# LayerNorm scales a unit two units behind its squares, and the gates are computed for a whole pair of images

## The chip, the core and the metric

The kernel runs on one core of a Trainium2 chip. The metric is the time of one execution in microseconds of the device. Five engines take part, each with its own instruction queue: TensorE (PE), VectorE (DVE), ScalarE (ACT), GpSimd (POOL) and SyncE (SP), which here only issues transfers (DMA). The engines wait for each other through semaphores.

## The reference

The program computes two layers in float32 on an input of 32 images with 128 channels and 56 x 56 pixels (100,352 tokens). Only the first layer matters here. It ends in a mixture of eight experts, and the routing needs what the changed stage computes.

```python
x = conv_depthwise_7x7(input) + dw_bias          # NCHW, then one token per pixel
mu, var = x.mean(-1), x.var(-1)                  # over the 128 channels
x = (x - mu) / sqrt(var + 1e-6) * ln_gamma + ln_beta
logits = x @ Wg + bg                             # 8 experts
topv, topi = top_k(logits, 2)
wts = softmax(topv)
order = argsort(-wts[:, 0])                      # the tokens by the first weight
# each expert takes its first 15,680 tokens in that order, computes
# gelu(x @ W1 + b1) @ W2 + b2, and adds it, weighted, to its tokens
x = input + x + layer_scale * moe
```

The second layer (coordinate attention and a 3 x 3 convolution) follows and is not touched.

## The kernel before

The kernel runs in stages that follow each other: the depthwise convolution (up to 670 us), LayerNorm with the gates (694 to 1226 us), the routing of expert 0 (to 1327 us), the experts with the rest of the routing (to about 3320 us), and the second layer. The change touches the second stage only, L175 to L309.

**Units.** A pair of images has 6272 tokens, 49 on each of the 128 partitions. The 16 pairs are each cut into two units: unit (i, 0) has 24 tokens per partition and unit (i, 1) 25. One unit passes through these steps:

- `centre` (L211): with the first unit of a pair, SP loads the images of the next pair (`lnyt`, L216; two buffers). Then, in groups of three tokens, PE multiplies each token with `proj` (L227). That gives the centred token, 128 values, and its eight unscaled logits in one PSUM tile (`lnps`, eight buffers). ACT copies the group to `cen` in SBUF (L228, three buffers of one unit) and squares it: in unit (i, 0) one token at a time with a running sum into `var` (L232), in unit (i, 1) a group at a time into `sqs` (L234, one buffer).
- `spread` (L236): in unit (i, 1) DVE sums the squares (L239). POOL turns `var` into the reciprocal root `rstd` by two instructions (L240, L241).
- `normalise` (L243): DVE scales each token by `rstd` and gamma into the row buffer `xn` (L250, one instruction per token, four buffers of one unit) and the logits (L253, L254). Then it searches for the two best experts (L260 to L269): maximum, comparison, rank, second maximum. This is a chain in which nearly every instruction needs the one before it.
- `exp` (L272): one ACT instruction.
- `gates` (L276 to L292): ten more DVE instructions and the expert index (L288) write the weights into the row and the priorities into `prio` (L292). SP stores the rows in `acc_d` (L294).

**What sets the order.** The loop at L299 puts the steps of different units beside each other: in turn k it calls `centre` of unit k, `exp` of unit k-2, `normalise` of unit k-1, `spread` of unit k and `gates` of unit k-2. A scheduler then orders the instructions of each engine by its own estimate of when they can start, which mixes the steps of a turn; every engine works its queue strictly in that order. On DVE, the scheduler sets the scales of one unit between the search and the gates of another. Buffers add waits: a unit's copies to `cen` wait until the unit that had the buffer has been read by L253, and the first scale of a unit waits until the rows that lay in its `xn` buffer are stored.

**Behind the stage.** The routing counts over all of `prio` (L407), so it begins when the last L292 is done. POOL clears a tile for a zero fill of `acc_d` (L579) when the last rows have been stored.

Of the kernel before, what the change touches and what calls it, by code (L numbers as in the profile page):

```python
# [21 lines left out]
E = 8  # L22
CAP = int(1.25 * T / E)
FF = 4 * C
P = 128
# [20 lines left out]
def bc(ap, shape):  # L46
    return ap.to_broadcast(shape)
# [3 lines left out]
def moe_conv_then_coordatt_kernel(ctx: ExitStack, tc: tile.TileContext, a: dict, out: bass.AP):  # L51
# [122 lines left out]

    with ExitStack() as st:  # L175
        yp = st.enter_context(tc.tile_pool(name="lny", bufs=2))
        cp1 = st.enter_context(tc.tile_pool(name="lnc", bufs=3))
        xp = st.enter_context(tc.tile_pool(name="lnx", bufs=4))
        sp = st.enter_context(tc.tile_pool(name="lns", bufs=3))
        pp = st.enter_context(tc.tile_pool(name="lnp", bufs=8, space=PSUM))  # L180
        halves = ((0, TPP // 2), (TPP // 2, TPP))
        U = TPP - TPP // 2
        rank_e = sp.tile([P, E], F32, name="rank_e", bufs=1)
        for e in range(E):
            nc.gpsimd.memset(rank_e[:, e : e + 1], float(E - e))
        one_u = sp.tile([P, U], F32, name="one_u", bufs=1)
        nc.gpsimd.memset(one_u, 1.0)
        all_e = sp.tile([P, U], F32, name="all_e", bufs=1)
        nc.gpsimd.memset(all_e, float(E))
        yts = {}  # L190

        class Unit:
# [12 lines left out]
            def over_tokens(self, x):  # L205
                return bc(x.unsqueeze(1), [P, self.n, E])

            def over_experts(self, x):
                return bc(x.unsqueeze(2), [P, self.n, E])

            def centre(self):  # L211

                if self.h == 0:
                    for i in range(len(yts), min(self.i + 2, NPAIR)):
                        yt = yp.tile([C, 2, HW], F32, tag="yt", name=f"lnyt{i}")
                        nc.sync.dma_start(yt, y_d[2 * i : 2 * i + 2].rearrange("n c f -> c n f"))  # L216
                        yts[i] = yt.rearrange("c n f -> c (n f)").rearrange("c (p j) -> c j p", j=TPP)
                yf = yts[self.i]
                self.cen = self.tile(cp1, "cen", [P, U, C + E])
                self.var = self.tile(sp, "var")  # L220
                if self.h == 1:
                    self.sq = cp1.tile([P, U, C], F32, tag="sqs", name=f"sqs{self.nm}", bufs=1)[:, 0 : self.n]
                for g in range(0, self.n, 3):
                    m = min(3, self.n - g)
                    ps = pp.tile([P, 3, C + E], F32, tag="ps", name=f"lnps{self.nm}_{g}")
                    for j in range(m):
                        nc.tensor.matmul(ps[:, j, :], lhsT=yf[:, self.j0 + g + j, :], rhs=proj, start=True, stop=True)  # L227
                    nc.scalar.copy(self.cen[:, g : g + m, :], ps[:, 0:m, :])  # L228
                    if self.h == 0:
                        for j in range(m):  # L230
                            sq = sp.tile([P, C], F32, tag="sq", name=f"sq{self.nm}_{g}_{j}")
                            nc.scalar.activation(sq, ps[:, j, 0:C], AF.Square, accum_out=self.var[:, g + j : g + j + 1])  # L232
                    else:
                        nc.scalar.activation(self.sq[:, g : g + m, :], ps[:, 0:m, 0:C], AF.Square)  # L234

            def spread(self):  # L236
                self.rstd = self.tile(sp, "rstd")
                if self.h == 1:
                    nc.vector.tensor_reduce(self.var, self.sq, AX.X, ALU.add)  # L239
                nc.gpsimd.tensor_scalar(self.var, self.var, 1.0 / C, 1e-6, ALU.mult, ALU.add)  # L240
                nc.gpsimd.tensor_tensor(self.rstd, self.var, bc(mhalf, [P, self.n]), ALU.pow)  # L241

            def normalise(self):  # L243

                n = self.n
                self.row = self.tile(xp, "xn", [P, U, RW])
                xn = self.row[:, :, 0:C]
                rstd = self.rstd
                for j in range(n):
                    nc.vector.scalar_tensor_tensor(xn[:, j, :], self.cen[:, j, 0:C], rstd[:, j : j + 1], gamma_bc,  # L250
                                                   ALU.mult, ALU.mult)
                l = self.tile(sp, "lgs", [P, U, E])
                nc.vector.tensor_tensor(l, self.cen[:, :, C : C + E], self.over_experts(rstd), ALU.mult)  # L253
                nc.vector.tensor_tensor(l, l, self.over_tokens(logit_c), ALU.add)  # L254
                t = self.tile(sp, "gt", [P, U, E])
                self.oh = [self.tile(sp, f"oh{k}", [P, U, E]) for k in range(2)]
                self.m = [self.tile(sp, f"m{k}") for k in range(2)]
                self.later, second = self.tile(sp, "later"), self.tile(sp, "second")
                for k in range(2):
                    nc.vector.tensor_reduce(self.m[k], l, AX.X, ALU.max)  # L260
                    nc.vector.tensor_tensor(t, l, self.over_experts(self.m[k]), ALU.is_equal)
                    nc.vector.tensor_tensor(t, t, self.over_tokens(rank_e), ALU.mult)
                    mx = (self.later, second)[k]
                    nc.vector.tensor_reduce(mx, t, AX.X, ALU.max)
                    nc.vector.tensor_tensor(self.oh[k], self.over_tokens(rank_e), self.over_experts(mx), ALU.is_equal)
                    if k == 0:
                        nc.vector.scalar_tensor_tensor(l, self.oh[0], -3.0e38, l, ALU.mult, ALU.add)
                nc.vector.tensor_tensor(self.m[1], self.m[1], self.m[0], ALU.subtract)
                nc.vector.tensor_tensor(self.later, self.later, second, ALU.min)  # L269

            def exp(self):
                nc.scalar.activation(self.m[1], self.m[1], AF.Exp)  # L272

            def gates(self):

                n, mx, w0, w1 = self.n, self.m[1], self.tile(sp, "w0"), self.tile(sp, "w1")  # L276
                one = one_u[:, 0:n]
                t = self.tile(sp, "gt2", [P, U, E])
                nc.vector.tensor_tensor(mx, mx, one, ALU.min)
                nc.vector.tensor_tensor(w0, mx, one, ALU.add)  # L280
                nc.vector.reciprocal(w0, w0)
                nc.vector.scalar_tensor_tensor(w0, w0, 0.5, one, ALU.max, ALU.min)
                nc.vector.tensor_tensor(w1, mx, w0, ALU.mult)
                row, oh = self.row, self.oh
                nc.vector.tensor_tensor(row[:, :, C : C + E], oh[0], self.over_experts(w0), ALU.mult)
                nc.vector.tensor_tensor(t, oh[1], self.over_experts(w1), ALU.mult)
                nc.vector.tensor_tensor(row[:, :, C : C + E], row[:, :, C : C + E], t, ALU.add)
                nc.vector.scalar_tensor_tensor(row[:, :, C + E : RW], self.later.unsqueeze(2), -1.0,  # L288
                                               all_e[:, 0:n].unsqueeze(2), ALU.mult, ALU.add)
                nc.vector.tensor_tensor(oh[1], oh[0], oh[1], ALU.add)  # L290
                cols = slice(self.i * TPP + self.j0, self.i * TPP + self.j1)
                nc.vector.tensor_tensor(prio[:, :, cols].rearrange("p e t -> p t e"), oh[1], self.over_experts(w0), ALU.mult)  # L292
                rows = slice(self.i * TPP * P, (self.i + 1) * TPP * P)
                nc.sync.dma_start(acc_d[rows, :].rearrange("(p j) c -> p j c", p=P)[:, self.j0 : self.j1, :], row)  # L294

        mhalf = sp.tile([P, 1], F32, name="mhalf", bufs=1)
        nc.gpsimd.memset(mhalf, -0.5)
# [12 lines left out]


    with ExitStack() as st:
# [759 lines left out]
```

## Time and profile before

| what | us |
|---|---|
| median of 3 runs | 4523.59 (4507.34 to 4524.99) |
| the profiled execution | 4519.41 |
| its span, first to last instruction | 4517.7 |
| first matmul of the stage | 694.48 |
| first scale of a token | 711.38 |
| last write of `prio` begins | 1225.72 |
| first gather of expert 0 | 1326.92 |
| first scatter of expert 0 | 1387.58 |

The page gives the busy time of each engine over the whole span: PE 3625.3 us (80%), DVE 2569.1 (57%), POOL 2550.8 (56%), ACT 1411.3 (31%). These shares are means over stages that differ. For one stage, the windows view gives the busy time of each engine between two times, with the number of instructions in brackets, the granted clock of PE, the share of the transfer engines and the rate in GB/s. The timeline gives, per instruction, its start, its duration, the engine, the line of the kernel, the operation, what it writes and reads, and in square brackets how long the engine had been idle and what released it. On one engine an instruction can start before the record of the one before it ends, so the distance of two starts is the time that an instruction costs, and the duration is a little more.

### The profile page before, as it was taken

Reading aid. Unit: us, or ns where it says so; the run is one execution under the profiler, and the core shown is the slowest. Engines: PE = TensorE matmul, PEld = TensorE weight load, DVE = VectorE, ACT = ScalarE, POOL = GpSimd, SP = SyncE. Lnnn points to the kernel's source line nnn. Section 1 sums busy time; section 2 is a strip of 40 time slices with the busy share of each in tenths; the row PEclk is TensorE's granted clock in tenths of the full one; section 3 lists DMA queues with packets and bytes.
Section 4 is the critical chain, followed back from the end, with each engine's and each line's share of the span. In section 5 each row is a group of like instructions: output and inputs, shape, how many; then the busy total and the mean of one; then the engine's idle time right before and its main releaser. Section 6 shows DMA issues by size and latency. Waiting matters only on the chain. (4 is left out here: it accounts for less than half of the span.)

```text
span 4517.7 us, 59987 instructions
## 1 busy us (share of the span) xinstructions
PE 3625.3 (80%) x21360; PEld 2369.6 (52%) x21360; DVE 2569.1 (57%) x5914; ACT 1411.3 (31%) x3132; POOL 2550.8 (56%) x1983
## 2 busy tenths in 40 slices
PE   9999998676328896788788446697958999999899
PEld 4555448676316665565565334464634544455444
DVE  1111115888866966886743112232358888888786
ACT  1111115555203432334243222343412333333232
POOL 1000102232217777668677437777769787877775
PEclk9999998787658898798898778898979999999999
DMA  9999995545362121111111111111155555555552
GB/s 172 217 230 216 230 192 195 231 183 236 150 230 56 49 59 51 44 44 46 52 52 56 46 34 52 56 56 56 56 164 187 174 191 194 168 190 171 176 161 77
DMA packets 814971, 587.33 MB, mean 130 GB/s; under 512 B 545984, under 2 KB 751312, under 8 KB 802128
## 3 DMA queue, kind: packets, MB, share of 16 engines
q1 hardware_dynamic: 508816, 328.72, 25.3%
q10 hardware_dynamic: 262336, 157.84, 12.4%
q0 software_dynamic: 43264, 94.64, 7.3%
q8 instruction: 193, 3.16, 0.3%
q14 instruction: 362, 2.97, 0.2%
HBM read 320.96 MB, written 260.09 MB: 129 GB/s over the span
## 5 line engine op out<-in xcount | busy, mean ns | idle before, releaser
L591 POOL DMA_INDIRECT xg<-acc_d,idx x676 | 673.1, 996 | 408.7 <-issue 172.5
L646 POOL DMA_INDIRECT acc_d<-yo,row x676 | 717.1, 1061 | 234.8 <-issue 82.8
L612 PE MATMUL ph<-fxt,w 128*128 128x512 f32 (+1 forms) x1440 | 700.8, 631 | 53.7 <-ACT ht L613 53.7
L613 ACT ACTIVATE ht<-ph,bias 128x512 f32<-128x512 f32 (+1 forms) x720 | 489.5, 682 | 703.7 <-PE ph L612 702.6
L977 PE MATMUL pc<-v,wk 128*128 128x392 f32 x1920 | 706.1, 510 | 0.4 <-POOL v L962 0.4
L621 PEld LDWEIGHTS py<-w,ht 128*128 128x128 f32 x5728 | 664.9, 192 | 64.8 <-issue 58.2
L621 PE MATMUL py<-w,ht 128*128 128x128 f32 x5728 | 670.5, 276 | 0.0
L144 PE MATMUL acc<-xt,band 56*64 56x424 f32 (+3 forms) x7168 | 666.5, 528 | 2.7 <-POOL band L132 2.7
L144 PEld LDWEIGHTS acc<-xt,band 56*64 56x64 f32 x7168 | 337.6, 133 | 331.0 <-issue 273.3
L977 PEld LDWEIGHTS pc<-v,wk 128*128 128x128 f32 x1920 | 349.2, 192 | 308.6 <-issue 105.7
L227 PE MATMUL lnps<-proj,lnyt 128*128 128x136 f32 x1568 | 354.7, 400 | 138.8 <-ACT sq L232 71.8
L612 PEld LDWEIGHTS ph<-fxt,w 128*128 128x128 f32 x1440 | 279.5, 206 | 329.0 <-issue 243.1
L636 ACT ACTIVATE yo<-xg,own 128x137 f32<-128x137 f32 x716 | 238.0, 401 | 634.9 <-DVE own L632 369.6
L227 PEld LDWEIGHTS lnps<-proj,lnyt 128*128 128x128 f32 x1568 | 349.4, 319 | 144.6 <-ACT sq L232 74.5
L157 DVE TENSOR_SCALAR yt<-acc,dwb 128x448 f32<-128x448 f32 x128 | 87.5, 684 | 582.2 <-PE acc L144 425.2
L639 DVE TENSOR_TENSOR ys<-py,b 128x512 f32<-128x512 f32 (+2 forms) x184 | 123.8, 675 | 490.8 <-PE py L621 480.8
L602 PE MATMUL pt<-ident,xg 128*128 128x128 f32 x716 | 137.0, 311 | 329.7 <-issue 159.2
L132 POOL COPY band<-hk 56x392 f32<-56x392 f32 x128 | 65.2, 510 | 572.4 <-issue 502.0
L987 DVE SCALAR_TENSOR_TENSOR y<-pc,y 128x392 f32<-128x392 f32 x640 | 317.6, 554 | 17.7 <-PE pc L977 17.6
L957 POOL TENSOR_TENSOR d<-pad 128x3248 f32<-128x3248 f32 x32 | 228.1, 7127 | 171.2 <-DVE pad L949 171.2
L894 POOL TENSOR_TENSOR cxn<-cxn,cx 128x896 f32<-128x896 f32 x112 | 261.5, 2344 | 68.3 <-DMA cxn<-acc_d 24.5
L602 PEld LDWEIGHTS pt<-ident,xg 128*128 128x128 f32 x716 | 96.3, 161 | 357.9 <-issue 311.2
(225 smaller groups left out, 4653.8 us busy)
## 6 DMA issues: line engine op xcount, KB each, us to landing
xt<-in_x SPq DMA_DIRECT2D x128, 392.0 KB
y_d<-yt ACTq DMA_DIRECT2D x256, 196.0 KB
lnyt<-y_d SPq DMA_DIRECT2D x16, 3136.0 KB
x<-in_x SPq DMA_DIRECT2D x16, 3136.0 KB
cxn<-acc_d SPq DMA_DIRECT2D x112, 448.0 KB
cx<-acc_d SPq DMA_DIRECT2D x112, 448.0 KB
out<-y ACTq DMA_DIRECT2D x64, 784.0 KB
acc_d<-xn SPq DMA_DIRECT2D x16, 1712.5 KB
```

What stands on the lines that cost most here:

```text
L144: nc.tensor.matmul(acc[c][half * G : (half + 1) * G, :, lo:hi], lhsT=band[rows, dw, :], rhs=xt[rows, im, lo + s : hi + s], start=(n == 0), ...
L227: nc.tensor.matmul(ps[:, j, :], lhsT=yf[:, self.j0 + g + j, :], rhs=proj, start=True, stop=True)
L591: d = nc.gpsimd.indirect_dma_start(out=xg[0:n, k, :], out_offset=None, in_=acc_d[0:T1, :], in_offset=bass.IndirectOffsetOnAxis(ap=idx[0][0 ...
L602: nc.tensor.transpose(pt[:, k * P : k * P + n], xg[0:n, k, 0:C], ident[0:n, 0:n])
L612: nc.tensor.matmul(ph[:, 0:N_], lhsT=w[0][:, f * P : (f + 1) * P], rhs=xt[:, 0:N_], start=True, stop=True)
L613: nc.scalar.activation(ht[:, f, 0:N_], ph[:, 0:N_], AF.Gelu, bias=w[2][:, f : f + 1])
L621: nc.tensor.matmul(py[0:n, k, :], lhsT=ht[:, f, k * P : k * P + n], rhs=w2[:, f, :], start=(f == 0), stop=(f == NF - 1))
L636: nc.scalar.activation(yo[0:n, k, :], xg[0:n, k, :], AF.Copy, scale=own[0:n, k : k + 1])
L646: d = nc.gpsimd.indirect_dma_start(out=acc_d[:, :], out_offset=bass.IndirectOffsetOnAxis(ap=row[0:n, k : k + 1], axis=0), in_=yo[0:n, k, : ...
L894: nc.gpsimd.tensor_tensor(xn, xn, x2, ALU.add)
L977: nc.tensor.matmul(m[k], lhsT=wk[k][:, dw, :], rhs=v[:, k, rows, dw : dw + W], start=(dw == 0), stop=(dw == 2))
L987: nc.vector.scalar_tensor_tensor(r[x], m[k], f, r[y_], ALU.mult, ALU.add)
```

## The change

- `normalise` of a unit is called two turns behind its `centre` and `spread` instead of one. `cen` has four buffers instead of three.
- The search and the gates are moved from the class `Unit` to a class `Pair` and work on all 49 tokens of a pair at once: the search in the turn behind, the gates one turn later. Their work tiles have one buffer each instead of three.
- The row buffer holds a pair, in two buffers (four of one unit before), and the rows of a pair are stored by one transfer.
- The single squares of ACT share one buffer `sq` instead of three. `sqs` moves to a pool of its own, with one buffer as before.
- The loop runs one turn longer.

The core of the diff, with the calls of the loop:

```diff
-        cp1 = st.enter_context(tc.tile_pool(name="lnc", bufs=3))
-        xp = st.enter_context(tc.tile_pool(name="lnx", bufs=4))
+        cp1 = st.enter_context(tc.tile_pool(name="lnc", bufs=4))
+        qp = st.enter_context(tc.tile_pool(name="lnq", bufs=1))
+        xp = st.enter_context(tc.tile_pool(name="lnx", bufs=2))
...
+        class Pair:
+            def tile(self, pool, tag, shape=None):
+                return pool.tile(shape or [P, TPP], F32, tag=tag, name=f"{tag}{self.i}", bufs=2 if pool is xp else 1)
+            def open(self):
+                self.row = self.tile(xp, "xn", [P, TPP, RW])
+                self.l = self.tile(sp, "lgs", [P, TPP, E])
+            def top(self):
+                l, n = self.l, TPP
+                nc.vector.tensor_tensor(l, l, over_tokens(logit_c, n), ALU.add)
...
+            def gates(self):
...
+                nc.sync.dma_start(acc_d[rows, :].rearrange("(p j) c -> p j c", p=P), row)
...
-                            sq = sp.tile([P, C], F32, tag="sq", name=f"sq{self.nm}_{g}_{j}")
+                            sq = sp.tile([P, C], F32, tag="sq", name=f"sq{self.nm}_{g}_{j}", bufs=1)
...
             def normalise(self):
...
+                pair = pairs[self.i]
+                if self.h == 0:
+                    pair.open()
+                for j in range(self.n):
+                    nc.vector.scalar_tensor_tensor(pair.row[:, self.j0 + j, 0:C], self.cen[:, j, 0:C],
+                                                   self.rstd[:, j : j + 1], gamma_bc, ALU.mult, ALU.mult)
+                nc.vector.tensor_tensor(pair.l[:, self.j0 : self.j1, :], self.cen[:, :, C : C + E],
+                                        over_experts(self.rstd, self.n), ALU.mult)
...
-        for k in range(len(units) + 2):
+        for k in range(len(units) + 3):
+            pair = pairs[(k - 3) // 2] if k >= 3 else None
             if k < len(units):
                 units[k].centre()
-            if k >= 2:
-                units[k - 2].exp()
-            if 1 <= k <= len(units):
-                units[k - 1].normalise()
+            if pair and k % 2 == 0:
+                pair.exp()
             if k < len(units):
                 units[k].spread()
-            if k >= 2:
-                units[k - 2].gates()
+            if 2 <= k <= len(units) + 1:
+                units[k - 2].normalise()
+            if pair:
+                (pair.top if k % 2 else pair.gates)()
```

In the changed kernel the first line of the search is L218, the gates' last write of the row is L250, the reduction is L303, the scale L312 and the logits L314. The bodies of `top` and `gates` hold the same instructions as before, over 49 tokens.

More of the change, by code (lines that the diff above doesn't have):

```diff
@@ L182, in moe_conv_then_coordatt_kernel @@
         U = TPP - TPP // 2
+        NSQ = TPP // 2
         rank_e = sp.tile([P, E], F32, name="rank_e", bufs=1)
@@ L185, in moe_conv_then_coordatt_kernel @@
             nc.gpsimd.memset(rank_e[:, e : e + 1], float(E - e))
-        one_u = sp.tile([P, U], F32, name="one_u", bufs=1)
-        nc.gpsimd.memset(one_u, 1.0)
-        all_e = sp.tile([P, U], F32, name="all_e", bufs=1)
+        one_t = sp.tile([P, TPP], F32, name="one_t", bufs=1)
+        nc.gpsimd.memset(one_t, 1.0)
+        all_e = sp.tile([P, TPP], F32, name="all_e", bufs=1)
         nc.gpsimd.memset(all_e, float(E))
+        mhalf = sp.tile([P, 1], F32, name="mhalf", bufs=1)
+        nc.gpsimd.memset(mhalf, -0.5)
@@ L190, in moe_conv_then_coordatt_kernel, with over_tokens, over_experts, __init__ @@
         yts = {}
+        def over_tokens(x, n):
+            return bc(x.unsqueeze(1), [P, n, E])
+        def over_experts(x, n):
+            return bc(x.unsqueeze(2), [P, n, E])
+        class Pair:
+            def __init__(self, i):
+                self.i = i
+            def tile(self, pool, tag, shape=None):
[6 more added lines that the diff above has]
+                nc.vector.tensor_tensor(l, l, over_tokens(logit_c, n), ALU.add)
+                t = self.tile(sp, "gt", [P, TPP, E])
+                self.oh = [self.tile(sp, f"oh{k}", [P, TPP, E]) for k in range(2)]
+                self.m = [self.tile(sp, f"m{k}") for k in range(2)]
+                self.later, second = self.tile(sp, "later"), self.tile(sp, "second")
+                for k in range(2):
+                    nc.vector.tensor_reduce(self.m[k], l, AX.X, ALU.max)
+                    nc.vector.tensor_tensor(t, l, over_experts(self.m[k], n), ALU.is_equal)
+                    nc.vector.tensor_tensor(t, t, over_tokens(rank_e, n), ALU.mult)
+                    mx = (self.later, second)[k]
+                    nc.vector.tensor_reduce(mx, t, AX.X, ALU.max)
+                    nc.vector.tensor_tensor(self.oh[k], over_tokens(rank_e, n), over_experts(mx, n), ALU.is_equal)
+                    if k == 0:
+                        nc.vector.scalar_tensor_tensor(l, self.oh[0], -3.0e38, l, ALU.mult, ALU.add)
+                nc.vector.tensor_tensor(self.m[1], self.m[1], self.m[0], ALU.subtract)
+                nc.vector.tensor_tensor(self.later, self.later, second, ALU.min)
+            def exp(self):
+                nc.scalar.activation(self.m[1], self.m[1], AF.Exp)
+            def gates(self):
+                n, mx, w0, w1 = TPP, self.m[1], self.tile(sp, "w0"), self.tile(sp, "w1")
+                t = self.tile(sp, "gt", [P, TPP, E])
+                nc.vector.tensor_tensor(mx, mx, one_t, ALU.min)
+                nc.vector.tensor_tensor(w0, mx, one_t, ALU.add)
+                nc.vector.reciprocal(w0, w0)
+                nc.vector.scalar_tensor_tensor(w0, w0, 0.5, one_t, ALU.max, ALU.min)
+                nc.vector.tensor_tensor(w1, mx, w0, ALU.mult)
+                row, oh = self.row, self.oh
+                nc.vector.tensor_tensor(row[:, :, C : C + E], oh[0], over_experts(w0, n), ALU.mult)
+                nc.vector.tensor_tensor(t, oh[1], over_experts(w1, n), ALU.mult)
+                nc.vector.tensor_tensor(row[:, :, C : C + E], row[:, :, C : C + E], t, ALU.add)
+                nc.vector.scalar_tensor_tensor(row[:, :, C + E : RW], self.later.unsqueeze(2), -1.0, all_e.unsqueeze(2),
+                                               ALU.mult, ALU.add)
+                nc.vector.tensor_tensor(oh[1], oh[0], oh[1], ALU.add)
+                cols = slice(self.i * TPP, (self.i + 1) * TPP)
+                nc.vector.tensor_tensor(prio[:, :, cols].rearrange("p e t -> p t e"), oh[1], over_experts(w0, n), ALU.mult)
+                rows = slice(self.i * TPP * P, (self.i + 1) * TPP * P)
+                nc.sync.dma_start(acc_d[rows, :].rearrange("(p j) c -> p j c", p=P), row)
@@ L192, in moe_conv_then_coordatt_kernel @@
+        pairs = [Pair(i) for i in range(NPAIR)]
         class Unit:
@@ L203, in tile @@
                 return t[:, 0 : self.n]
[L205 to L209, printed above, removed]
             def centre(self):
@@ L220, in centre @@
                 self.var = self.tile(sp, "var")
-                if self.h == 1:
-                    self.sq = cp1.tile([P, U, C], F32, tag="sqs", name=f"sqs{self.nm}", bufs=1)[:, 0 : self.n]
+                self.alone = 0 if self.h else NSQ
+                if self.alone < self.n:
+                    self.sq = qp.tile([P, U, C], F32, tag="sqs", name=f"sqs{self.nm}")
                 for g in range(0, self.n, 3):
@@ L228, in centre @@
                     nc.scalar.copy(self.cen[:, g : g + m, :], ps[:, 0:m, :])
-                    if self.h == 0:
+                    if g < self.alone:
                         for j in range(m):
-                            sq = sp.tile([P, C], F32, tag="sq", name=f"sq{self.nm}_{g}_{j}")
+                            sq = sp.tile([P, C], F32, tag="sq", name=f"sq{self.nm}_{g}_{j}", bufs=1)
                             nc.scalar.activation(sq, ps[:, j, 0:C], AF.Square, accum_out=self.var[:, g + j : g + j + 1])
@@ L237, in spread @@
                 self.rstd = self.tile(sp, "rstd")
-                if self.h == 1:
-                    nc.vector.tensor_reduce(self.var, self.sq, AX.X, ALU.add)
+                if self.alone < self.n:
+                    nc.vector.tensor_reduce(self.var, self.sq[:, 0 : self.n], AX.X, ALU.add)
                 nc.gpsimd.tensor_scalar(self.var, self.var, 1.0 / C, 1e-6, ALU.mult, ALU.add)
@@ L243, in normalise @@
             def normalise(self):
[L245 to L294, printed above, removed]
@@ L296, in moe_conv_then_coordatt_kernel @@
-        mhalf = sp.tile([P, 1], F32, name="mhalf", bufs=1)
-        nc.gpsimd.memset(mhalf, -0.5)
+                pair = pairs[self.i]
[6 more added lines that the diff above has]
+                                        over_experts(self.rstd, self.n), ALU.mult)
```

## The prediction

> **What bounds the kernel now.** The stage between the depthwise convolution and the routing, 694.5 to 1226.1 us, is the only one whose code changes. It ends when the last write of `prio` (L292, 1225.72 + 0.4) lets the routing count begin. First view: busy time by window, for the stage and for one period of it, a pair of images (two units of 24 and 25 tokens).
>
> ```profile
> core 0: us, PE busy (x) PEld busy (x) DVE busy (x) ACT busy (x) POOL busy (x), PEclk, DMA share, GB/s
> 694.48:1226.14 531.66, 356.57 (x1576) 351.19 (x1576) 447.96 (x1645) 270.98 (x1216) 150.59 (x82) 0.78 0.48 193
> ...
> 820.63:852.52 31.89, 22.30 (x99) 21.90 (x99) 27.84 (x103) 16.77 (x76) 9.21 (x4) 0.73 0.52 210
> ```
>
> Read the second line: a pair takes 31.89 us; DVE works 27.84 of them, PE 22.30, ACT 16.77, POOL 9.21. DVE bounds it and loses 4.05 us. Where, says DVE's timeline around the pair's border, and POOL's beside it:
>
> ```profile
> 812.26 3.49 DVE L239 TENSOR_REDUCE var<-sqs 128x25 f32<-128x3200 f32 x1
> 815.65 0.35 DVE L254 TENSOR_TENSOR lgs<-lgs,logit_c 128x192 f32<-128x192 f32 x1
> ...
> 816.42 0.17 DVE L280 TENSOR_TENSOR w<-m,one_u 128x25 f32<-128x25 f32 x1
> 820.63 0.35 DVE L250 SCALAR_TENSOR_TENSOR xn<-cen,rstd,gamma_bc 128x128 f32<-128x128 f32 x1 [4.05 <-POOL rstd L241]
> ```
>
> ```profile
> 815.83 0.38 POOL L240 TENSOR_SCALAR var<-var 128x25 f32<-128x25 f32 x1 [22.43 <-DVE var L239]
> 816.29 4.31 POOL L241 TENSOR_TENSOR rstd<-var,mhalf 128x25 f32<-128x25 f32 x1
> 820.68 0.37 POOL L240 TENSOR_SCALAR var<-var 128x24 f32<-128x24 f32 x1
> 821.14 4.15 POOL L241 TENSOR_TENSOR rstd<-var,mhalf 128x24 f32<-128x24 f32 x1
> ```
>
> DVE sums the squares (L239), POOL needs 0.38 + 4.31 us for the root, and the scale (L250) that wants it stands a few instructions behind. The list of waits gives the same wait 100.5 us in 17 times: 33.9 at the stage's start, about 4.2 in each pair.
>
> **The change part by part.**
>
> *Scale two units behind.* In the built program's order, the reduction of unit (p+2, 1) now stands in the gates of pair p, a whole pair ahead of its scale. The 4.7 us of POOL lie beside some 27 us of DVE work: -4.05 per pair. Its cover would have to shrink below 4.7 us to bring any of it back.
>
> *Gates for a pair at once.* 25 instructions per unit (12 wide and 2 narrow in the search, 5 wide, 5 narrow and the expert index in the gates) become 25 per pair, twice as wide. DVE starts: 200 elements 0.273 us after the last, 192 0.265, 25 elements 0.09, 3200 elements 3.39 (812.26 to 815.65). So about 1.04 ns an element and 0.065 us per instruction: 25 x 0.065 = -1.6 us per pair.
>
> *What the order adds.* Before, the scheduler put a scale or a gate between most dependent instructions. After, ten of the pair's search (its first to its tenth wide instruction) directly follow the one they need. The routing's chain shows the price:
>
> ```profile
> 1228.01 0.16 DVE L419 TENSOR_SCALAR enough_r<-ps_r 128x1 f32<-128x1 f32 x1 [0.66 <-PE ps_r L408]
> 1228.09 0.14 DVE L421 TENSOR_SCALAR mid_r<-thr_r 128x1 f32<-128x1 f32 x1
> ...
> 1230.31 0.16 DVE L419 TENSOR_SCALAR enough_r<-ps_r 128x1 f32<-128x1 f32 x1 [0.68 <-PE ps_r L408]
> 1230.50 0.16 DVE L420 TENSOR_TENSOR thr_r<-thr_r,enough_r 128x1 f32<-128x1 f32 x1
> ```
>
> An independent neighbour starts 0.08 later, a dependent one 0.19: its predecessor's end and 0.03. A wide one shows the same (L254 at 1215.87 for 0.36, L260 at 1216.27). So 10 x 0.12 = +1.2 us per pair; bounds 0 and 25 x 0.12 = 3.0. The Trainium skill (VectorE: DVE Perf Modes, The DRAIN you can't avoid) says that a semaphore between chained Vector instructions costs nothing extra; by it this term would be 0 and the whole 4442. I keep the rows.
>
> The period is then 27.84 - 1.6 + 1.2 = **27.4 us** instead of 31.9.
>
> *Does another engine become the bound?* POOL's two roots, 9.2 us, now run wholly beside DVE. The second of them does already (821.14 to 825.29), and there DVE's two-input instructions start 0.26 to 0.28 apart as elsewhere: price 0, upper bound the 8.5 us of both. The Trainium skill (SBUF — State Buffer, Who interferes with whom) says that a Vector instruction with two SBUF inputs and a GpSimd instruction that reads SBUF lock each other out; by it up to 8.5 us per pair would come back, 14.5 x 8.5 = 123, and the whole would be an estimated 4583. The row speaks against it.
>
> PE needs 0.442 us a token (244 records, 122 tokens, in the 53.94 us from 694.48), 21.7 a pair. It waits for PSUM: ACT may copy a unit only when one of four `cen` buffers is free. With L314 of (p, 0) at 0 and of (p, 1) at 13.7, ACT copies and squares (p+2, 0) from 0, and PE refills eight groups by 13.4; those of the next unit are full 12.3 after 13.7, when 13.7 are there. So PE fits, by 0.3 us once. ACT's single squares now share one buffer: back to back, each waits for the last (0.16 to issue, 0.20 to 0.22 to read the sum, 0.04) and takes 0.40 instead of 0.25; 16 of 24 do, +2.4, in ACT's 15 idle us. The exponential waits in ACT's queue ahead of one copy and its squares, for a DVE result that comes 6 us after the unit's copies start; ACT has just finished them.
>
> *The rows leave pair by pair.* SP sends 3.44 MB at once instead of 1.68 and 1.75, and two pair buffers replace four unit buffers. The first scale of pair p+1 waits for the rows of pair p-1. DVE work from their last write (L250 new) to it: 0.47 + 0.26 + 0.53 + 21 x 0.263 + 0.40 + 9 x 0.60 + 1.1 = 13.7 us. Landing: the last rows before (1.75 MB) were issued at 1225.42 and released POOL at 1232.22, 6.8 us; the queues move 432 GB/s in the window 800 to 809, 4.1 us for 1.75 MB, so about 2.7 of latency. For 3.44 MB: 8.0 + 2.7 = 10.7. No wait, 3 us spare. In SP's queue the next image load comes behind the rows; it waits for PE's last matmul of pair p+3, thus for L314 of (p+1, 1), 7.1 us behind the rows' last write, and copies and squares after it, 8.8 in all, when the rows are nearly out.
>
> *The start costs.* ACT's new order mixes the first unit's squares with the second unit's copies, paced by PE: the last square comes behind the seventh copy of unit (0, 1), at 714.62 before, so it ends at about 715.5, and the first scale stands 4.7 us behind (706.7 to 711.4 before): 720.2. Then 5 scales, a reduction, 44 scales and the first wide ones take 17.5 (737.7); pair 1's squares end at 694.5 + 98 x 0.442 + 0.6 = 738.4; their reduction, the first search and 24 scales take 15.5 (754.0). The exponential, in ACT's queue behind work that PE paces, holds DVE to some 755.5. Pair 2's squares end after 147 tokens, 694.5 + 65.0 + 0.5 = 760.0, and its reduction, which DVE reaches at about 756.4, waits for them. From there the period rules.
>
> *The sum.* Reduction of pair 2 at 760.0; of pair 15, 13 periods later, 1116.2; one period on, 1143.6, DVE stands where the next would be, and needs 10.0 us (25 scales 6.6, five wide 2.5, the rest 0.9) to the last logits, 1153.6. Then the last pair's search, 12 wide at 0.58 with routing set-up between them (7.0), and gates with the b2 product of 1.14 (5.9): 1166.5. Before it was 1226.1: **-59.6 us**. Behind it the order on every engine is the same but for the set-up; the zero fill starts some 4 us later against `prio`, with the first scatter at 1387 and thus about 75 us spare. All of it shifts. The profiled execution took 4519.4 us (span 4517.7): 4459.8. The median of the runs is 4.2 above it; I say **4460**.
>
> **The rivals.**
>
> *A better one (4442).* Dependence costs nothing: period 26.2, 14.5 x 1.2 = 17 us more. For it: most dependent neighbours in the trace are one element long, and nothing says that long ones pay as much. Against: the PE margin of 0.3 us, which a shorter period eats.
>
> *A part comes back (4475 to 4505).* PE's refill or the image load late by 1 to 3 us in each pair: 14 x (1 to 3) = 14 to 42 us. For it: PE waited twice in each pair before:
>
> ```profile
> 807.01 15.30 PE L227 MATMUL lnps<-proj,lnyt 128*128 128x136 f32 x68 [5.64 <-ACT sq L232]
> 826.34 6.99 PE L227 MATMUL lnps<-proj,lnyt 128*128 128x136 f32 x30 [4.03 <-ACT sqs L234]
> ```
>
> *The change doesn't do what it says (4505 to 4523).* The scale finds a root that is late for another reason, or the start and the fuller tail eat it. Only if a pair still costs over 31 us.
>
> *Slower (4525 to 4567).* The row buffers: if the rows share the queues with the next image load (3.21 MB), both together need 6.65 / 0.432 = 15.4, + 2.7 = 18.1 us. From 13.7 + 4.5 = 18.2 on, the new wait of the first scale in a pair is as long as the old one. At the 361 GB/s that the window 1225 to 1300 shows, it is 18.4 + 2.7 = 21.1: a wait of 7.4, period 34.8, 14.5 x 2.9 + 5 = 47 us on top, 4567. Against it: the order and the 8.8 us above.
>
> **How the numbers follow.** Forecast (4445 to 4475) 0.62; better (4430 to 4445) 0.12; part comes back 0.16, of it 0.04 above 4497; doesn't do it 0.05; slower 0.05. About 0.5%, 23 us, is what a measurement here can tell from no change: faster is below 4497, 0.62 + 0.12 + 0.12 = 0.86; the same 0.09; slower 0.05. The range holds the forecast, three quarters of the better case and two thirds of the part that comes back, 0.62 + 0.09 + 0.11 = 0.82: 4434 to 4495; it takes in the 3.0 us bound of the dependence, 1.8 x 14.5 = 26 on top, 4486.
>
> **What would show it.** A DVE period of 27.4 us with no wait for `rstd` behind the start; the search's wide instructions 0.60 apart; no wait of the scale for the rows' DMA; the first scale at 720; the count at 1166. Wrong: a period set by PE, or a scale that DMA releases.

## The result, and the profile after

| | before | after |
|---|---|---|
| median of the runs, us | 4515.47 (4 runs, 4502.84 to 4524.99) | 4465.74 (4 runs, 4459.73 to 4468.19) |
| the profiled execution's span | 4517.7 | 4466.5 |
| first matmul of the stage | 694.5 | 694.1 |
| first scale of a token | 711.4 | 719.8 |
| last reduction of squares (pair 15) | 1195.9 | 1117.0 |
| the routing count begins | 1226.2 | 1169.4 |
| the stage: first matmul to count | 531.7 | 475.3 |

The ratio after to before is 0.9883, interval 0.9859 to 0.9906. The change makes the kernel faster by 50 us in the medians and by 56 us in the stage that it touches.

Busy time by window, for the stage and for one period of it, as it was shown for before (columns: window, its length, then busy time and instructions of each engine):

```profile
core 0: us, PE busy (x) PEld busy (x) DVE busy (x) ACT busy (x) POOL busy (x), PEclk, DMA share, GB/s
694.07:1169.40 475.33, 366.06 (x1576) 352.17 (x1576) 437.71 (x1249) 288.96 (x1200) 171.16 (x84) 0.81 0.53 214
842.39:869.86 27.47, 23.20 (x98) 21.97 (x98) 27.13 (x80) 18.16 (x76) 10.79 (x4) 0.88 0.60 242
```

A pair now takes 27.47 us instead of 31.89. DVE works 27.13 of them and has lost its 4 us of idle time. It starts 77 instructions in the period instead of 102, the 25 fewer that the change takes away (the 80 and 103 in the brackets also count those that the window's ends cut). Over thirteen periods, from the reduction of pair 2 to that of pair 15, the mean is (1116.96 - 760.56) / 13 = 27.42 us; before it was (1195.94 - 780.24) / 13 = 31.98.

DVE's timeline around a pair's border answers to the two views of before that showed the wait:

```profile
1089.50 3.48 DVE L303 TENSOR_REDUCE var<-sqs 128x25 f32<-128x3200 f32 x1
...
1093.97 0.55 DVE L248 TENSOR_TENSOR xn<-oh,w 128x392 f32<-128x392 f32 x1
1094.44 0.55 DVE L249 TENSOR_TENSOR gt<-oh,w 128x392 f32<-128x392 f32 x1
...
1095.18 0.55 DVE L250 TENSOR_TENSOR xn<-xn,gt 128x392 f32<-128x392 f32 x1
...
1097.07 5.57 DVE L312 SCALAR_TENSOR_TENSOR xn<-cen,rstd,gamma_bc 128x128 f32<-128x128 f32 x21
1102.56 0.35 DVE L314 TENSOR_TENSOR lgs<-cen,rstd 128x200 f32<-128x200 f32 x1
1102.95 0.57 DVE L218 TENSOR_TENSOR lgs<-lgs,logit_c 128x392 f32<-128x392 f32 x1
1103.55 0.56 DVE L224 TENSOR_REDUCE m<-lgs 128x49 f32<-128x392 f32 x1
1104.15 0.57 DVE L225 TENSOR_TENSOR gt<-lgs,m 128x392 f32<-128x392 f32 x1
```

No line has a bracket behind it: nothing waits. The reduction (L303) belongs to a unit whose scales come a whole pair later. The search begins at L218, and its instructions, each of which needs the one before it, start 0.60 us apart. The gates' L248 and L249, as wide but independent of each other, start 0.47 apart. The list of DVE's waits over the stage (columns: who waits for what, us in all, times, longest) has no steady-state wait left:

```profile
DVE xn L312 <- POOL rstd L305: 42.7, 2, 42.5
DVE var L303 <- ACT sqs L298: 6.1, 2, 4.5
```

The 42.5 us are the stage's start. The rest is two short waits for squares there (1.66 and 4.46 us) and one of 0.24 for a root.

### The profile page after: what moved, and what is told of

Its sections match the earlier page's. It is cut to its first block, busy times and chain, and to the rows that moved or that the text cites. A ratio compares the mean times of both kernels' runs of the same rounds, so it can differ in the third digit from the quotient of the medians.

```text
span 4466.5 us, 59526 instructions
## 1 busy us (share of the span) xinstructions
PE 3636.8 (81%) x21360; PEld 2379.5 (53%) x21360; DVE 2557.9 (57%) x5514; ACT 1429.9 (32%) x3116; POOL 2578.7 (58%) x1983
## 5 line engine op out<-in xcount | busy, mean ns | idle before, releaser
L291 PE MATMUL lnps<-proj,lnyt 128*128 128x136 f32 x1568 | 364.2, 399 | 63.9 <-ACT sq L296 39.2
L915 POOL TENSOR_TENSOR cxn<-cxn,cx 128x896 f32<-128x896 f32 x112 | 260.8, 2338 | 69.3 <-PE pc L998 26.4
```

Of the source, the lines that this page charges most:

```text
L915: nc.gpsimd.tensor_tensor(xn, xn, x2, ALU.add)
```

## The experiments

The experiments ran on three chips, numbered 3, 5 and 14 in the record, each with its own runs of the kernel before; by their times, none is the chip of the runs above. There the stages behind the count take much longer (the kernel before: 5050 to 5060 us), but the changed stage takes the same time: 475.1 us for the changed kernel on chip 14, against 475.3 above. So the stage is compared across all runs, and the whole only against the kernel before on the same chip (ratio, with its 95% interval). "Period" is the mean of thirteen pairs, as above.

| kernel | stage, us | period | whole against before, interval |
|---|---|---|---|
| before | 531.7 | 31.98 | 1 |
| after (chip 14) | 475.1 | 27.41 | 0.9896 (0.9866 to 0.9926) |
| moved scale alone | 478.2 | 27.84 | 0.9892 (0.9853 to 0.9931) |
| pairs alone | 487.1 | 28.10 | 0.9907 (0.9878 to 0.9936) |
| reduction moved alone | 471.1 | 27.76 | 0.9886 (0.9858 to 0.9914) |
| search between the scales | 494.4 | 28.82 | 0.9917 (0.9892 to 0.9942) |
| the same, late reduction and products | 464.1 and 463.1 | 26.99 and 26.91 | 0.9887 (0.9842 to 0.9932) and 0.9880 (0.9856 to 0.9904) |
| late products | 473.4 | 27.42 | 0.9897 (0.9866 to 0.9928) |
| root twice | 475.4 | 27.42 | one run, no interval |
| products on GpSimd (second try) | 542.8 | 32.16 | one run, no interval |
| rows twice | 545.0 | 33.09 | one run, no interval |

**The moved scale alone.**

```diff
# on the kernel before
-        cp1 = st.enter_context(tc.tile_pool(name="lnc", bufs=3))
+        cp1 = st.enter_context(tc.tile_pool(name="lnc", bufs=4))
...
-        for k in range(len(units) + 2):
+        for k in range(len(units) + 3):
...
-                units[k - 2].exp()
-            if 1 <= k <= len(units):
-                units[k - 1].normalise()
+                units[k - 3].exp()
             if k < len(units):
                 units[k].spread()
...
+                units[k - 2].normalise()
+            if k >= 3:
+                units[k - 3].gates()
```

> The kernel before with one part of the change: normalise and gates of a unit one turn later, four cen buffers; search and gates stay per unit, the rows leave per unit (single squares share one buffer as in the change, and the two scratch tiles of search and gates have one buffer, for room). Theory (the moved scale is the gain, the pairs are worth only 0.4 us): no wait of the scale for rstd behind the start, DVE period per pair 27.8 us, first scale at about 720, count at about 1172, whole 4460 to 4475. Rival (the pairs for themselves are the gain): wait of about 4 us stays, period near 31.9, whole near 4515.

Measured: period 27.84, one wait for `rstd` (42.8, the start), stage 478.2. The theory holds: the deferral takes all of the wait away, and the pairs add only 27.84 - 27.42 = 0.4 us per pair.

**The pairs alone.**

```diff
# on the changed kernel: cen bufs=3, the loop back to one turn of delay
+            if 1 <= k <= len(units):
+                units[k - 1].normalise()
             if k < len(units):
                 units[k].spread()
-            if 2 <= k <= len(units) + 1:
-                units[k - 2].normalise()
             if pair:
-                (pair.top if k % 2 else pair.gates)()
+                (pair.gates if k % 2 else pair.top)()
```

> The changed kernel with normalise one turn behind again and three cen buffers; search, gates and rows per pair as in the change. By its order the reduction of a unit (p+2, 1) still stands ahead of a whole pair's search and 24 scales, some 13 us ahead of its own scale, since the scheduler moves it there, and seven of the ten dependent neighbours of the search get a scale between them. Theory A (the wait goes wherever 4.7 us of DVE work stand between reduction and scale, whatever moved it): no wait for rstd in the steady state, period 26.6 to 27.0, count 1150 to 1165, whole 4448 to 4465. Theory B (the scale two units behind is what removes the wait): wait of about 4 us, period 31 to 31.9, whole 4500 to 4520.

Neither theory is right as it stood. The period is 28.10, far below 31.9; but seven waits for the root remain, 28.3 us in all, in the steady state one in every three pairs. DVE's timeline shows one:

```profile
931.68 3.48 DVE L303 TENSOR_REDUCE var<-sqs 128x25 f32<-128x3200 f32 x1
...
935.31 0.21 DVE L243 TENSOR_TENSOR w<-m,one_t 128x49 f32<-128x49 f32 x1
939.89 0.35 DVE L312 SCALAR_TENSOR_TENSOR xn<-cen,rstd,gamma_bc 128x128 f32<-128x128 f32 x1 [4.37 <-POOL rstd L305]
```

The reductions come in a pattern of three pairs (26.6, 40.0 and 18.1 us apart). In some pairs the scheduler sets the reduction far ahead of its scales, in others, as here, right in front of them. The wait goes where work lies between the two, and without the deferral that is left to the scheduler.

**The reduction moved alone.** If only that distance counts, the kernel before needs neither a fourth buffer nor pairs. One order on DVE is enough:

```diff
# on the kernel before
-            if 1 <= k <= len(units):
-                units[k - 1].normalise()
             if k < len(units):
                 units[k].spread()
+            if 1 <= k <= len(units):
+                units[k - 1].normalise(units[k].total if k < len(units) else None)
...
# in normalise: the scales of unit (p, 0) come behind the reduction of unit (p, 1)
+                    if total is not None:
+                        tc.add_manual_dep(scale.ins, total.ins.name, NOSYNC, reason="order on DVE alone")
```

> The kernel before with one thing moved and nothing else: on DVE the reduction of unit (p, 1) stands ahead of the scales of unit (p, 0) instead of ahead of its own; scales still one turn behind, three cen buffers, search, gates and rows per unit. Theory (all that counts is that 24 scales lie between reduction and scale, not the deferral as such): no wait for rstd, period 27.85 as with the moved scale alone, first matmul to count 475 to 482 us (before 531.7, moved scale alone 478.2), whole 1.0 to 1.2% below the kernel before. Rival (the fourth buffer is needed): the reduction waits for the squares instead, 1 to 4 us per pair, period 29 to 32, stage 495 to 530.

DVE's windows view of one period of this kernel (columns as above), then POOL's timeline in it:

```profile
824.72:852.50 27.78, 22.55 (x98) 21.88 (x98) 27.78 (x104) 16.47 (x78) 9.09 (x4) 0.88 0.63 240
```

```profile
828.29 0.21 POOL L242 TENSOR_SCALAR var<-var 128x25 f32<-128x25 f32 x1 [17.55 <-DVE var L241]
828.59 4.47 POOL L243 TENSOR_TENSOR rstd<-var,mhalf 128x25 f32<-128x25 f32 x1
```

DVE is busy for all of 27.78 us. The root is ready at 833.06; by DVE's timeline the scales of the other unit end with their logits at 839.38, and the unit's own scales follow. The theory holds, and the stage, 471.1 us, is even 4 us shorter than that of the full change. The period is 0.35 longer, but from the first scale to the last both kernels take the same 433.9 us, and the end is cheaper: from the last scale to the count it takes 1167.8 - 1156.7 = 11.1 us, in the changed kernel on the same chip 1174.6 - 1159.1 = 15.5, since there a search over 49 tokens stands alone behind the last scale.

**The search between the scales.**

```diff
# on the changed kernel: top() yields eleven of its twelve wide instructions (the first, L218, is not tied);
# the loop calls it one turn later, beside the scales of the next pair's first unit
                 for j in range(self.n):
...
+                    step = next(steps, None)
+                    if step is not None:
+                        tc.add_manual_dep(step.ins, scale.ins.name, NOSYNC, reason="order on DVE alone")
```

> The changed kernel with each of the twelve wide search instructions of a pair set behind one scale of the next unit on DVE, so that no wide one follows the one that it needs; same instructions, same buffers. If a dependent neighbour costs 0.12 us more than an independent one: starts of the pair's search instructions 0.48 after their predecessor's end of turn, period 27.4 - 10 x 0.12 = 26.2, 14.5 x 1.2 = 17 us less than the changed kernel, 4449. If dependence costs nothing and 0.60 is the price of their shape: period 27.4 as in the change, 4466. If PE's refill becomes the bound (margin 0.3 us): period 26.8 to 27.1.

Measured: period 28.82 in the mean, 28.24 in most pairs. DVE's timeline where a search begins:

```profile
1006.99 0.57 DVE L218 TENSOR_TENSOR lgs<-lgs,logit_c 128x392 f32<-128x392 f32 x1
1009.38 0.35 DVE L314 SCALAR_TENSOR_TENSOR xn<-cen,rstd,gamma_bc 128x128 f32<-128x128 f32 x1 [1.82 <-DMA acc_d<-xn]
1009.64 0.55 DVE L224 TENSOR_REDUCE m<-lgs 128x49 f32<-128x392 f32 x1
1010.12 0.34 DVE L314 SCALAR_TENSOR_TENSOR xn<-cen,rstd,gamma_bc 128x128 f32<-128x128 f32 x1
1010.37 0.56 DVE L225 TENSOR_TENSOR gt<-lgs,m 128x392 f32<-128x392 f32 x1
```

Two things are to be seen. A wide search instruction now costs 1010.12 - 1009.64 = 0.48 us instead of 0.60, so a dependent neighbour does cost 0.12. That speaks against the Trainium skill (VectorE: DVE Perf Modes, The DRAIN you can't avoid) where it would make the chain free. Nor is the 0.12 a matter of shape, for in the changed kernel the gates' L248 and L249, as wide and independent, start 0.47 apart. And the bracket shows the wait that the prediction's slower rival named: the first scale of a pair now stands in front of most of the search and waits for the rows' transfer. The work between the rows' last write (ends at 999.76) and that scale fell from 13.7 to 7.8 us, and the rows landed after 9.6. All three periods of the expectation missed for that reason: 28.24 - 1.82 = 26.4 is the work.

**The same, with the reduction and the weight products later.**

```diff
+                    if self.i >= 2:      # the reduction behind the gates of pair p-2
+                        tc.add_manual_dep(total.ins, pairs[self.i - 2].last.ins.name, NOSYNC, reason="order on DVE alone")
```

> The kernel with the search between the scales and, besides, the reduction of the squares set behind the gates' last write of prio instead of ahead of the gates (3.4 us), and GpSimd's weight products behind the last gates. The rows of a pair then leave 3.4 us earlier against the next pair's first scale. Theory (with the search between, the period was 26.4 of work and 1.8 of wait for the rows): no wait of the scale for the rows, period 26.4, 13.5 x 1.0 = 14 us less than the changed kernel in the stage, first matmul to count 459 to 463 us (changed kernel 475.3, search between the scales alone 494.4). Rival (PE or ACT cannot keep up with less than 27 us, since squares and reduction come later): DVE waits for sqs or rstd instead, period 27 to 28.

> The kernel with the search between the scales, the late reduction and the late weight products again, beside the changed kernel on one chip: first matmul to count 462 to 465 us, so 10 to 13 us below the changed kernel in the stage and, if nothing behind it takes it back, in the whole; if the stages behind wander by more than that, the medians differ by less and only the stage shows it.

Most periods are 26.28 us, with no wait. What remains of the rows' wait is 8.7 and 7.9 us in the whole stage, 6.4 and 6.8 of it in one early pair. The stage takes 464.1 and 463.1 us, 11 to 12 below the 475.1 of the changed kernel: the best stage of all. In the whole, 4991.77 us median (4975.76 to 5006.19) against 4999.01 (4977.04 to 5023.09) on the same chip, the two cannot be told apart.

**The late products.**

```diff
+            if e < 2:       # the first experts' products wait for the last write of prio
+                after(scaled.ins, ln_pairs[-1].last.ins, "GpSimd's product behind the last gates")
```

> The changed kernel with one wait added: GpSimd's two products of the first experts' weights (128x512, 1.33 and 1.26 us) wait for the last write of prio instead of running beside the last pair's gates. Theory (the two DVE instructions that grew beside them, 0.24 to 1.31 us and 0.20 to 1.03 us, were held by GpSimd): both are back at 0.2, the way from the last logits to the count falls from 15.0 by 1.9 to 13.1 us, the rest is as in the changed kernel, period 27.4. Rival (they grew for another reason, as a late operand): they stay, 15.0 us. A whole of 2 us less can't be told in the median; the profile decides.

The changed kernel's DVE and POOL timelines at the end of the stage, then DVE's of this kernel:

```profile
1162.52 1.31 DVE L251 SCALAR_TENSOR_TENSOR xn<-later,all_e 128x49 f32<-128x49 f32 x1
...
1164.21 1.03 DVE L245 SCALAR_TENSOR_TENSOR w<-w,one_t 128x49 f32<-128x49 f32 x1
```

```profile
1162.39 1.33 POOL L687 TENSOR_TENSOR w<-w,ls_bc 128x512 f32<-128x512 f32 x1 [4.04 <-DMA w<-in_W]
1163.91 1.26 POOL L687 TENSOR_TENSOR w<-w,ls_bc 128x512 f32<-128x512 f32 x1 [0.18 <-DMA w<-in_W]
```

```profile
1171.07 0.25 DVE L251 SCALAR_TENSOR_TENSOR xn<-later,all_e 128x49 f32<-128x49 f32 x1
...
1171.68 0.21 DVE L245 SCALAR_TENSOR_TENSOR w<-w,one_t 128x49 f32<-128x49 f32 x1
```

Both DVE instructions ended just after the POOL product beside them (1163.83 and 1163.72; 1165.24 and 1165.17). Without the products they are short again, the way from the last logits to the count takes 1176.1 - 1163.0 = 13.1 us instead of 15.0, and the stage is 1.7 to 1.9 us shorter. So a GpSimd product does hold DVE.

**GpSimd beside DVE: the root twice, and products instead.**

```diff
# root twice
+                idle = self.tile(sp, "idle")
+                nc.gpsimd.tensor_tensor(idle, self.var, bc(mhalf, [P, self.n]), ALU.pow)
# products, second try
+                for _ in range(3):
+                    nc.gpsimd.tensor_tensor(wide[:, 0, :], wide[:, 1, :], bc(self.rstd[:, 0:1], [P, 4 * C]), ALU.mult)
```

> The changed kernel with the reciprocal root of each unit computed a second time on GpSimd into a tile that nobody reads: 4.15 to 4.46 us more of GpSimd per unit, 8.7 per pair, beside DVE's two-input instructions. Theory (the root itself holds DVE up for nothing): period 27.4 to 27.6. By the rule of the Trainium skill (SBUF — State Buffer, Who interferes with whom) that a GpSimd instruction that reads SBUF and a two-input Vector instruction shut each other out for a whole instruction, an estimate of up to 8.7 more, 36 us.

> The changed kernel with three products of 128x512 from SBUF on GpSimd behind each unit's root, into a tile that nobody reads: as much GpSimd time per pair as a second root (6 x 1.26 = 7.6 us) but all of it streaming. Theory (a streaming GpSimd instruction holds a two-input Vector instruction, as the weight products held 1.9 us in 2.6): period longer by 7.6 x 1.9 / 2.6 = 5.5 us, 33 us, upper end 35, or, where DVE's run of scales wins, GpSimd's products grow to several us each instead and the period grows less, to 29 to 33. Rival (no lock between the two): period 27.4, products 1.26 each.

> The changed kernel with three products of 128x512 on GpSimd behind each unit's root, which read rstd and so cannot run ahead of it (the first try ran them in the convolution instead). Theory (a streaming GpSimd instruction that runs holds a two-input DVE instruction to its end, while a run of such DVE instructions holds GpSimd): DVE instructions of up to 1.3 us beside products, 0 to 1.3 us lost for each, period 28.5 to 34; products that begin in a run of 19 or more scales take 3 to 6 us instead of 1.26. Rival (no lock): period 27.46, products 1.26 each.

The second root cost nothing: period 27.42. The first try with products was lost: nothing in the stage held them there, the scheduler set all 96 into the convolution, the stage began at 791.4 us and itself took 475.3. In the second try the period grew to 32.16, by 4.7 us for 7.0 us of products (3.68 + 3.29). DVE's and POOL's timelines at the same time:

```profile
1041.03 0.56 DVE L226 TENSOR_REDUCE m<-lgs 128x49 f32<-128x392 f32 x1
1041.63 1.33 DVE L227 TENSOR_TENSOR gt<-lgs,m 128x392 f32<-128x392 f32 x1
1042.99 1.29 DVE L228 TENSOR_TENSOR gt<-gt,rank_e 128x392 f32<-128x392 f32 x1
```

```profile
1036.95 4.47 POOL L307 TENSOR_TENSOR rstd<-var,mhalf 128x24 f32<-128x24 f32 x1 [4.03 <-DVE lgs L318]
1041.50 3.68 POOL L309 TENSOR_TENSOR wide<-wide,rstd 128x512 f32<-128x512 f32 x3
```

Beside the root (to 1041.42) DVE keeps its pace, and L226 takes 0.56. Beside the products L227 and L228 take 1.3 instead of 0.57. Next to the changed kernel, the whole loss of such a pair, 4.8 us, sits in six DVE instructions, as many as there are products: three of the search and three scales, 0.7 to 0.9 us each. What the expectation said of products in a run of scales happened to two of the 96 (5.08 and 6.06 us), not as a rule: the run of 21 scales took 8.08 us instead of 5.6, so the two took turns.

**The rows twice.**

```diff
                 nc.sync.dma_start(acc_d[rows, :].rearrange("(p j) c -> p j c", p=P), row)
+                nc.sync.dma_start(acc_d[rows, :].rearrange("(p j) c -> p j c", p=P), row)
```

> The changed kernel with the rows of each pair stored twice, one transfer behind the other (the second writes the same values again), so that the rows' buffer is free later. The last rows of the changed kernel took 11.4 us to land; a second copy is estimated at 8.0 + 2.7 behind them, more if it shares the queues with the images: 22 to 30 us against 13.7 us of DVE work. If the first scale of a pair waits for the rows as the rival on the slower side has it: a wait of 8 to 16 us in front of the first scale of a pair, released by the transfer, period 36 to 43, whole 4585 to 4690. If the rows never hold the scale: period 27.4, whole 4466.

This one did not test what it was made for. The scheduler answered the longer transfer with another order: all 49 scales of a pair in one run, and no wait for a transfer in the list. The period is 33.09. POOL's timeline, then DVE's beside it, show why:

```profile
1034.76 0.21 POOL L305 TENSOR_SCALAR var<-var 128x25 f32<-128x25 f32 x1 [3.88 <-DVE var L304]
1044.45 11.19 POOL L306 TENSOR_TENSOR rstd<-var,mhalf 128x25 f32<-128x25 f32 x1 [9.47 <-DVE xn L313]
```

```profile
1037.93 12.94 DVE L313 SCALAR_TENSOR_TENSOR xn<-cen,rstd,gamma_bc 128x128 f32<-128x128 f32 x49
...
1055.66 0.37 DVE L315 TENSOR_TENSOR lgs<-cen,rstd 128x200 f32<-128x200 f32 x1 [3.70 <-POOL rstd L306]
```

The root begins inside the run of scales (1037.93 to 1050.87) and takes 11.19 us instead of 4.31. It ends 3.7 us after DVE's last instruction of that stretch, while DVE waits for it. Its usual 4.31 us before its end at 1055.64 is 1051.33, just behind the run; so it looks held by DVE's run of two-input instructions until then. This wait and another of 0.93 for a root are 4.6 of the 5.9 us by which most pairs are longer (33.36 against 27.46).

## Why the prediction was right, point by point

- **The bound and the wait.** Right: the wait of 4.05 us is gone, and both the moved scale alone (27.84) and the moved reduction alone (27.76) come to the 27.84 us of busy time that the prediction read. What it did not see is that the deferral is not needed for it.
- **Pairs, -1.6, and dependence, +1.2.** Right in the sum: -0.4 predicted, 27.42 - 27.84 = -0.42 measured. The parts are supported too: the search starts 0.60 apart in the change and 0.48 with scales between, and where that search runs without a wait for the rows, most periods are 26.28, against 27.84 - 1.6 = 26.24. The better rival (dependence for nothing) falls.
- **The period.** 27.4 predicted, 27.42 measured.
- **POOL beside DVE, price 0.** Right for what it was said of, the root: twice the root, the same period. But "the row speaks against it" went too far. The lock that the Trainium skill describes (SBUF — State Buffer, Who interferes with whom) exists here: products of 128x512 hold DVE, and a run of scales holds GpSimd. Already in the changed kernel POOL's L304 takes 1.81 us beside the run of 21 scales instead of 0.22. Only the root escapes the half of the rule that holds DVE up for the whole instruction. L304 passes over as many columns in 0.22 us where nothing holds it, so most of the root's 4.3 us can hardly be reading. That this is the reason is argued, not shown: no run here has a root as wide as the products.
- **PE and ACT.** Right: behind the start DVE never waits for squares, and PE's waits (3.3, 0.2 and 0.5 us a pair) stay beside DVE's work. Back to back, the single squares take 0.40 us as predicted (696.25, 696.66, 697.06).
- **The rows.** Right: no wait. The room is 13.7 us, as predicted (1123.2 to 1136.9); the last rows took 1179.51 - 1168.07 = 11.4 to land, against 10.7. The slower rival has a real mechanism: with 7.8 us of room it costs 1.8 us in each pair. Its own condition, a landing of 18.2 us, was never reached and remains untested.
- **The start.** Right: first scale at 719.8 (predicted 720.2), reduction of pair 2 at 760.6 behind a wait of 4.5 for squares (760.0), of pair 15 at 1117.0 (1116.2), last logits at 1154.4 (1153.6).
- **The end of the stage.** The step that was mis-sized: "the last pair's search [...] (7.0), and gates [...] (5.9)", 12.9 us. It took 1169.4 - 1154.4 = 15.0. Of the 2.1 missing, GpSimd's weight products, which now fall beside the last gates (in the kernel before they ran behind them, at 1226.7 and 1233.6), are 1.07 + 0.83 = 1.9. The sum had no term for them. With the products held back, the same way takes 13.1.
- **Behind the stage, all shifts.** The count begins 56.8 us earlier, the first gather 56.9, but the span is 51.2 shorter. In the two profiled executions the same DVE instruction of the experts' stage (its code is the same) stands 56.5 us earlier at 1323 us, 53.2 at 1918, 56.4 at 2655 and 50.5 at 3227: the distance goes up and down. On chip 14 the medians differ by 5055.6 - 4999.0 = 56.6, all of the shift. That the missing 5.6 us are the wandering of that stage is supported by this, not shown.

So 4460 was 5.7 us too low for the median. The gain was further off: 59.6 us forecast, 51.2 between the two profiled executions, with 2.8 missing in the stage and 5.6 behind it. That the median came closer is luck: the forecast named the 4.2 us by which the median before lay above the profiled execution and did not add them, and after the change the median (4465.74) lies 2.5 below the profiled execution (4468.19). Between the medians the gain is 49.7 us, by the interval 42 to 64.

## What to carry to other kernels

A wait of an in-order engine for its own result by way of another engine is a matter of distance in its queue; move the producer forward before buying buffers, for here one order constraint gave as much as the whole change (stage 471.1 against 475.1 us). When you take work from between two ends, list which other waits that work covered: putting the search between the scales saved 1 us of work and uncovered 1.8 us of waiting for the rows. Fixing an order that the scheduler only happened to choose is part of such a change, and a test whose instructions can be moved must tie them to their place.

## What the runs showed of the hardware that was not expected

- GpSimd and two-input DVE instructions hold each other, but not by the length of the record: a product of 128x512 from SBUF (1.04 to 1.33 us) makes a DVE instruction last as long as itself (0.24 to 1.31, 0.57 to 1.33), a root over 24 or 25 columns (4.2 to 4.5 us) does not slow DVE at all (period 27.42 with two roots a unit).
- The other way round, a back-to-back run on DVE can hold GpSimd: with the root doubled, GpSimd's multiply-add of 25 columns took 5.0 us instead of 0.22 beside 21 scales, and a root took 11.19 instead of 4.31 beside 49. But three products queued behind each other got into a run of 21 scales in most pairs (8.08 us instead of 5.6). What decides between the two, no run here shows.
